# Attention scores in one run per kind: four heads' exponentials first, four heads' maxima second

## The chip, the cores and the metric

The kernel runs on one core of one Trainium2 chip. The metric is the time of one execution in microseconds of the device, the median of several runs. Engines are named as in the profile: PE is the matrix engine, PEld its weight loads, DVE the vector engine, ACT the scalar engine, POOL the general-purpose engine, SP the queue that issues most DMAs.

## The reference

A transformer layer on `x` of shape (2, 1024, 512) in float32. First attention with 32 heads of 16 channels, then a feed-forward part with quantised weights (512 to 1376 to 512).

```python
x = x + attn(layernorm(x))      # q, k, v projections; per head:
                                #   scores = q @ k.T / 4        (1024 x 1024)
                                #   softmax(scores) @ v
                                # then the output projection w_o
x = x + ffn(layernorm(x))       # int4 input, ternary weights, relu(gate)^2 * up,
                                # int8 middle, down projection
```

Attention dominates: 2 x 32 matrices of 1024 x 1024 scores, each reduced to a softmax and multiplied with `v`.

## The kernel before

**Steps and slots.** One *step* is four heads of one batch entry and 512 queries; there are 32 steps. The four heads of a step stand in the four groups of 32 partitions (r = 0 to 3), so one head's score product has a contraction of 32 rows and uses a quarter of PE's rows. Products of different r can stand in the array at the same time. A step has eight *slots* (`NT = 8`), and the loop at L1400 goes through all slots of all steps, one slot T after the other.

**The scores are computed twice.** Once with queries on the partitions, so that DVE can take the maximum over keys ("maxima", `max_mm` L590, tile `psm`, reduced by DVE at L600 into `pm`); ten slots later (`LE = NT + 2`) with keys on the partitions, so that ACT can take the exponential ("exponentials", `exp_mm` L630, tile `pse`, ACT at L634 into `e`). The score product of the exponentials has three passes per head: two with the query's high and low part, and one that adds the row of maxima (`mrow`, out of `onesr`). The maxima have two passes per head. A slot does one tile of each for each of the four heads. A PSUM tile `pse` or `psm` holds two heads (128 x 1024 float32): j = 0 holds r = 0 and 1, j = 1 holds r = 2 and 3.

**The order of PE's work in a slot** is the order in which the program is written (manual schedule; each engine runs its instructions in order):

1. `scores(...)`, the *first run*,
2. `weigh_values` (L660): the exponentials of the slot before times `v`, eight matmuls,
3. `fill.run(100.0, short=True)`: light steps of other work, hardly ever a matmul,
4. `scores(...)`, the *second run*,
5. in the second slot of a step `max_rows` (L613, tile `psn`): the step's maxima turned into a row,
6. `fill.run(...)`: the *filler*, matmuls of the projections, the output projection and the feed-forward part, by a budget that is fixed when the program is built.

`scores` allocates its tiles and mixes the passes of both kinds:

```python
es = [(*x, scores_psum(f"pse_{x[0]}_{x[1]}_{x[2]}")) for x in exps]
ms = [(*x, max_tile(*x)) for x in maxs]
for l in range(3):
    for x in es:
        exp_mm(*x, l)
    if l or not es:
        for x in ms:
            max_mm(*x, l - bool(es)) if l - bool(es) < 2 else None
for x in es:
    exponentials(*x)      # ACT, L634
for x in ms:
    max_reduce(*x)        # DVE, L600
```

**Before the change**, a slot with both kinds ("mixed") makes its first run of the exponentials with j = 0 and the maxima with j = 1, and its second run of the exponentials with j = 1 and the maxima with j = 0. Each run has one tile for ACT and one for DVE. The slots T = 0 to 9 have maxima alone and the last ten have exponentials alone; those make one run of four heads.

**PSUM.** `scores_psum` takes from a pool of three tiles of two banks each (`ps_s`, `bufs=3`), in turn: each tile takes the place of the one three allocations earlier, and its first matmul waits until that one has been read. `psn` takes from the same pool. The filler has one bank of its own (`ps_o`), the accumulator of `weigh_values` another (`ps_a`).

**Other DVE and ACT work** stands in the same in-order queues, behind the filler matmuls that feed it: normalisation, quantisation of weights and activations, products of the feed-forward part. In the first slot of a step DVE also does `max_parts` (L605 to L608).

Of the kernel before, what the change touches and what calls it, by code (L numbers as in the profile page):

```python
# [233 lines left out]
def kernel(  # L234
# [101 lines left out]
    def scores_psum(name):  # L336
        return ps_s.tile([P, 2, QB], F32, tag="s", name=name)
# [224 lines left out]
    def places(n):  # L562
        kst[n] = sb.tile([P, S], F32R, tag="kst", name=f"kst_{n}", bufs=3)
        qst[n] = [sb.tile([P, QB], F32R, tag="qst", name=f"qst_{n}_{l}", bufs=6) for l in range(2)]

    def load_k(n, first=0):
        nc.sync.dma_start(kst[n][:, first:].bitcast(F32), step_k(n)[:, :, first:])

    def load_q(n):
        b, h, g, s = steps[n]  # L570
        for l, q in enumerate(qst[n]):
            rows = qD[b, g, h][l].rearrange("(r s e) q -> s r e q", r=4, s=2)[s]
            nc.sync.dma_start(q.bitcast(F32), rows)

    def load_v(n):
        b, h, g, s = steps[n]
        vt[n] = sb.tile([P, NT, 4, 32], F32, tag="v", name=f"v_{n}", bufs=2)
        nc.sync.dma_start(vt[n].rearrange("p t r e -> p (t r e)"), vD[b, g, s].rearrange("p t e -> p (t e)"))

    def max_tile(n, i, j):  # L580

        if i == 0 and n not in pm:
            pm[n] = sp.tile([P, TQ, 2, 4], F32, tag="pm", name=f"pm_{n}")
        return scores_psum(f"psm_{n}_{i}_{j}")

    def max_mm(n, i, j, ps, l):
        kh, t = divmod(i, TQ)
        for r in (2 * j, 2 * j + 1):
            rows = slice(32 * r, 32 * r + 32)
            nc.tensor.matmul(  # L590
                ps[:, r % 2, :],
                qst[n][l][rows, t * P : (t + 1) * P],
                kst[n][rows, kh * QB : (kh + 1) * QB],
                start=(l == 0),
                stop=(l == 1),
            )

    def max_reduce(n, i, j, ps):
        kh, t = divmod(i, TQ)
        nc.vector.tensor_reduce(pm[n][:, t, kh, 2 * j : 2 * j + 2], ps, AX.X, ALU.max, negate=True)  # L600

    def max_parts(n):
        m = sp.tile([P, TQ, 4], F32, tag="m", name=f"m_{n}")
        p = pm.pop(n)
        nc.vector.tensor_tensor(m, p[:, :, 0, :], p[:, :, 1, :], ALU.min)  # L605
        cols = mcols[n % 2].rearrange("p t (r c) -> p t r c", r=4)
        nc.vector.tensor_copy(cols[:, :, :, 0], m)
        nc.vector.tensor_tensor(cols[:, :, :, 1], m, cols[:, :, :, 0].bitcast(F32), ALU.subtract)  # L608
# [12 lines left out]
    def exp_mm(n, i, j, ps, l):  # L621
        for r in (2 * j, 2 * j + 1):
            rows = slice(32 * r, 32 * r + 32)
            if l < 2:
                left, right = kst[n][rows, i * P : (i + 1) * P], qst[n][l][rows, :]
            else:

                rows = slice(32 * r, 32 * r + 2)
                left, right = onesr[rows, :], mrow[n][rows, :]
            nc.tensor.matmul(ps[:, r % 2, :], left, right, start=(l == 0), stop=(l == 2))  # L630

    def exponentials(n, i, j, ps):
        e = sb.tile([P, 2, QB], F32, tag="e", name=f"e_{n}_{i}_{j}", bufs=4)
        nc.scalar.activation(e, ps, AF.Exp, scale=SCALE)  # L634
        probs.setdefault((n, i), {})[j] = e

    def scores(exps, maxs):
# [11 lines that stand above are left out]
            exponentials(*x)  # L649
        for x in ms:  # L650
            max_reduce(*x)
# [3 lines left out]
    def weigh_values(n, i):  # L655
        if i == 0:
            acc[n] = ps_a.tile([P, QB], F32, tag="a", name=f"pso_{n}")
        e = probs.pop((n, i))
        for r in range(4):
            nc.tensor.matmul(  # L660
                acc[n][32 * r : 32 * r + 32, :],
                vt[n][:, i, r, :],
                e[r // 2][:, r % 2, :],
                start=(i == 0),
                stop=(i == NT - 1),
            )
        if i == NT - 1:
            po[n] = sb.tile([P, QB], F32, tag="po", name=f"po_{n}", bufs=3)
            nc.scalar.copy(po[n], acc[n])

    def normalise(n):


        b, h, g, _ = steps[n]
        p0, p1 = po.pop(n - 1), po.pop(n)
        dD = dram.tile([4, 2, QB], F32, name=f"dD_{n}")
        rD = dram.tile([4, 2, QB], F32, name=f"rD_{n}")
        yield ("gap", 3)
        for s, p in enumerate((p0, p1)):
            nc.sync.dma_start(dD[:, s, :], p[16 * (1 - s) :: 32, :])  # L680
        yield ("gap", 4)
        k = 8 * QB // P
        den = sp.tile([P, k], F32, tag="den", name=f"den_{n}", bufs=2)
        nc.sync.dma_start(den, bass.AP(dD.tensor, dD.offset, [[k, P], [1, k]]))
        yield ("gap", 6)
        for c in (slice(0, QB // 2), slice(QB // 2, QB)):
            nc.vector.copy_predicated(p0[:, c], second.to_broadcast([P, QB // 2]), p1[:, c])
            yield ("gap", 1)
        nc.vector.reciprocal(den, den)
        yield ("gap", 2)  # L690
        nc.sync.dma_start(bass.AP(rD.tensor, rD.offset, [[k, P], [1, k]]), den)
        yield ("gap", 3)
        rden = sb.tile([P, QB], F32, tag="rden", name=f"rden_{n}", bufs=1)
        nc.sync.dma_start(
            rden, bass.AP(rD.tensor, rD.offset, [[QB, 8], [0, 16], [1, QB]])
        )
        yield ("gap", 4)
        OT[b, h, g] = sb.tile([P, QB], F32, tag="OT", name=f"OT_{b}_{h}_{g}", bufs=5)
        nc.gpsimd.tensor_tensor(OT[b, h, g], p0, rden, ALU.mult)  # L699
# [617 lines left out]
    def load_slot(n):  # L1317

        return NT * n - (4 if n == 2 else 5)
# [5 lines left out]
    def due_v(n):  # L1325
        return NT * n + (8 if n < 8 else 5)
# [64 lines left out]
    def feed():  # L1391

        while ffns and set(ffns[0][2]) <= fill.done | {ffns[0][2][0]}:
            name, gen, after, due, cost, by = ffns.popleft()
            fill.add(name, gen, after, "ffn", due, cost, by)
# [4 lines left out]
    for T in range(LE + NT * NSTEP + 1):  # L1400
        fill.slot = T
        ne, ie = divmod(T - LE, NT)
        nm, im = divmod(T, NT)
        nw, iw = divmod(T - LE - 1, NT)

        fill.scores = int(T < LE - 1 or T >= NT * NSTEP)

        n = T // NT + 1
        if 1 < n < NSTEP and T == load_slot(n):
            b, h, g, s = steps[n]  # L1410
            fill.ensure(f"k_{b}_{g}_0", f"k_{b}_{g}_1", f"q_{b}_{g}_{h}")
            places(n)
            load_k(n)
            load_q(n)
        n = (T - 5) // NT
        if 0 <= n < NSTEP and T == due_v(n):
            b, h, g, s = steps[n]
            fill.ensure(f"v_{b}_{g}_0", f"v_{b}_{g}_1")
            load_v(n)
        if im == 0 and 0 < nm <= NSTEP:  # L1420
            max_parts(nm - 1)
        exps = [(ne, ie, j) for j in range(2)] if 0 <= ne < NSTEP else []
        maxs = [(nm, im, j) for j in (1, 0)] if nm < NSTEP else []
        mixed = bool(exps and maxs)
        if mixed:
            scores(exps[:1], maxs[:1])
        elif exps:
            scores(exps, [])
        if 0 <= nw < NSTEP:
            weigh_values(nw, iw)  # L1430
            if iw == NT - 1 and nw % 2 and nw < NSTEP - 1:
                b, h, g, _ = steps[nw]
                fill.add(f"norm_{b}_{h}_{g}", normalise(nw), (), "back")
            if iw == NT - 1 and nw == NSTEP - 2:
                fill.add("tokens", first_tokens(nw), (), "ffn", 0)
        feed()
        fill.run(100.0, short=True)
        if mixed:
            scores(exps[1:], maxs[1:])
        elif maxs:  # L1440
            scores([], maxs)
        if im == 1 and 0 < nm <= NSTEP:
            max_rows(nm - 1)
        share = min(max(fill.pace([w[4:] for w in ffns]), SHARE), MORE)
        left = fill.run(share + min(left, SHARE))
# [52 lines left out]
```

## Time and profile before

| | |
|---|---|
| time, three runs | 1177.97, 1178.94, 1180.83 us; median 1178.94 |
| profiled execution | span 1179.7 us from first to last instruction; the page gives no other time of it |
| PE busy | 1154.8 us, 98% of the span |
| DVE busy | 868.8 us, 74% |
| ACT busy | 686.8 us, 58% |
| POOL busy | 264.1 us, 22% |
| granted PE clock | 0.999 (mean) |

In the timeline a line gives start, length, engine, line of the kernel, instruction, tile written <- tiles read, shapes and number of instructions merged; the bracket is the idle time of the engine before it and what ended it. A matmul's length contains the time in which the next ones already run, so intervals are read from start to start.

### The profile page before, as it was taken

What the parts mean: (1) busy time and instruction counts of PE and PEld (TensorE: products, weight loads), DVE (VectorE), ACT (ScalarE), POOL (GpSimd) and SP (SyncE); (2) the same over time, 40 slices, a digit from 0 to 9 for tenths busy, and PEclk for the clock granted to TensorE, in tenths of its full rate; (3) what the DMA queues carried; (4) which work ended last, traced back from release to release, by engine and by line L of the source; (5) the groups of instructions that cost most, each with busy time, mean ns of one, the idle gap of its engine ahead of it and who ended that gap; (6) DMA issues with size and microseconds to landing.
All of it is one profiled execution on the core that took longest, in us unless ns stands there. A gap on an engine that the chain in (4) does not pass through costs nothing.

```text
span 1179.7 us, 21990 instructions
## 1 busy us (share of the span) xinstructions
PE 1154.8 (98%) x8922; PEld 522.5 (44%) x8922; DVE 868.8 (74%) x1261; ACT 686.8 (58%) x878; POOL 264.1 (22%) x319
## 2 busy tenths in 40 slices
PE   8899999999999999999999999999999999999998
PEld 5454444544444444544444445444444433444344
DVE  6765577898876677788866665786988788888467
ACT  2058765556565556566665555465666555665746
POOL 3224336465501101221011011022110001220111
PEclk9999999999999999999999999999999999999999
DMA  5666765556623323443633324244442516362300
GB/s 157 174 183 194 249 197 176 172 190 197 194 93 96 103 55 110 113 95 77 94 86 121 124 59 147 84 130 138 84 97 60 89 53 83 58 81 55 79 9 37
DMA packets 97099, 135.35 MB, mean 115 GB/s; under 512 B 34829, under 2 KB 54285, under 8 KB 96997
## 3 DMA queue, kind: packets, MB, share of 16 engines
q1 hardware_dynamic: 87204, 105.75, 34.6%
q0 software_dynamic: 9792, 28.19, 7.7%
q8 instruction: 70, 1.15, 0.4%
q14 instruction: 33, 0.26, 0.1%
HBM read 89.25 MB, written 37.19 MB: 107 GB/s over the span
## 4 chain that ended last, share of the span: by engine, by line
PE 81%; DVE 5%; DMA 5%; issue 2%; POOL 2%; SPq 2%; ACT 2%; POOLq 0%; DVEq 0%; ACTq 0%
PE pse L630 25%; PE pso L660 18%; PE psm L590 9%; PE psv L533 4%; PE psk L476 4%; PE psy L847 4%; PE psq L476 4%; PE pu L937 2%; PE py L1006 2%; DVE pm L600 2%; PE pg L937 2%; DMA rden<-rD 1%; PE psn L613 1%; SPq L505 1%; PE end L1161 1%
## 5 line engine op out<-in xcount | busy, mean ns | idle before, releaser
L600 DVE TENSOR_REDUCE pm<-psm 128x2 f32<-128x1024 f32 x512 | 623.8, 1222 | 242.9 <-PE pse L630 146.0
L634 ACT ACTIVATE e<-pse 128x1024 f32<-128x1024 f32 x512 | 522.7, 1023 | 408.2 <-PE pse L630 307.3
L590 PE MATMUL psm<-kst,qst 32*128 32x512 f32 x2048 | 369.5, 444 | 7.3 <-DMA kst<-kD 3.8
L630 PE MATMUL pse<-qst,kst 32*128 32x512 f32 x2048 | 367.6, 442 | 3.9 <-DVE pm L600 3.1
L630 PEld LDWEIGHTS pse<-qst,kst 32*128 32x128 f32 x2048 | 149.2, 183 | 332.8 <-issue 199.7
L660 PE MATMUL pso<-e,v 128*32 128x512 f32 x2048 | 272.9, 605 | 0.0
L630 PE MATMUL pse<-mrow,onesr 2*128 2x512 f32 x1024 | 203.9, 396 | 0.0
L590 PEld LDWEIGHTS psm<-kst,qst 32*128 32x128 f32 x2048 | 151.3, 183 | 25.5 <-ACT e L634 10.8
L630 PEld LDWEIGHTS pse<-mrow,onesr 2*128 2x128 f32 x1024 | 94.5, 183 | 3.3
L951 POOL TENSOR_TENSOR g<-g 128x460 f32<-128x460 f32 (+1 forms) x36 | 34.7, 964 | 244.7 <-ACT g L947 237.4
L660 PEld LDWEIGHTS pso<-e,v 128*32 128x32 f32 x2048 | 40.4, 108 | 94.4 <-issue 93.7
L807 POOL TENSOR_SCALAR low<-raws,whalf 128x512 bf16<-128x512 f32 (+2 forms) x35 | 52.0, 1488 | 30.5 <-DMA raws<-in_wuT 8.1
L476 PE MATMUL psq<-xnT,wq 128*128 128x512 f32 x112 | 57.8, 626 | 0.0
L533 PE MATMUL psv<-wv,xnT 128*128 128x128 f32 x384 | 53.2, 285 | 0.0
L533 PEld LDWEIGHTS psv<-wv,xnT 128*128 128x128 f32 x384 | 45.9, 191 | 12.5 <-issue 11.7
L847 PE MATMUL psy<-wo,OT 128*128 128x512 f32 x96 | 49.6, 625 | 0.0
L476 PE MATMUL psk<-xnT,wk 128*128 128x512 f32 x96 | 49.5, 624 | 0.0
L699 POOL TENSOR_TENSOR OT<-po,rden 128x512 f32<-128x512 f32 x15 | 19.2, 1278 | 99.5 <-PE pse L630 52.8
L547 POOL DMA_DIRECT2D vD<-vst x30 | 16.7, 559 | 110.5 <-ACT vst L545 107.8
L909 POOL TENSOR_SCALAR xn<-x,mv,a 128x512 f32<-128x512 f32 x12 | 25.1, 2089 | 71.5 <-DVE a L885 71.5
L937 PEld LDWEIGHTS <-xqT 128*128 128x128 bf16 x288 | 22.4, 98 | 37.8 <-issue 23.8
L937 PE MATMUL pg<-wg,xqT 128*128 128x460 fp8e4 (+1 forms) x144 | 34.2, 360 | 0.0
(227 smaller groups left out, 945.1 us busy)
## 6 DMA issues: line engine op xcount, KB each, us to landing
v<-vD SPq DMA_DIRECT2D x32, 512.0 KB
kst<-kD SPq DMA_DIRECT2D x31, 512.0 KB
qst<-qD SPq DMA_DIRECT2D x60, 256.0 KB
vD<-vst POOLq DMA_DIRECT2D x30, 256.0 KB, 5.7
qD<-hi_q SPq DMA_DIRECT2D x28, 256.0 KB
qD<-lo_q SPq DMA_DIRECT2D x28, 256.0 KB
x<-in_x SPq DMA_DIRECT2D x20, 256.0 KB
rden<-rD SPq DMA_DIRECT2D x15, 256.0 KB
```

The source lines that it names most:

```text
L476: nc.tensor.matmul(ps, w[:, c, :], xnT[b, h][:, c, :], start=(c == 0), stop=(c == KC - 1))
L533: nc.tensor.matmul(ps[:, i * P : (i + 1) * P], xnT[b, half][:, c, i * P : (i + 1) * P], w[:, c, :], start=(c == 0), stop=(c == KC - 1),)
L590: nc.tensor.matmul(ps[:, r % 2, :], qst[n][l][rows, t * P : (t + 1) * P], kst[n][rows, kh * QB : (kh + 1) * QB], start=(l == 0), stop=(l = ...
L600: nc.vector.tensor_reduce(pm[n][:, t, kh, 2 * j : 2 * j + 2], ps, AX.X, ALU.max, negate=True)
L630: nc.tensor.matmul(ps[:, r % 2, :], left, right, start=(l == 0), stop=(l == 2))
L634: nc.scalar.activation(e, ps, AF.Exp, scale=SCALE)
L660: nc.tensor.matmul(acc[n][32 * r : 32 * r + 32, :], vt[n][:, i, r, :], e[r // 2][:, r % 2, :], start=(i == 0), stop=(i == NT - 1),)
L807: nc.gpsimd.tensor_scalar(low, w, h[:rows, m, 1:2], None, ALU.is_lt)
L847: nc.tensor.matmul(ps, OT[b, h, g][:, i * P : (i + 1) * P], wo[g], start=(g == 0), stop=(g == NG - 1),)
L909: nc.gpsimd.tensor_scalar(xn, xt, mean, a, ALU.subtract, ALU.mult)
L937: nc.tensor.matmul(ps, xT[:, c, :], w[:, c, n : n + size], start=(c == 0), stop=(c == KC - 1))
L951: nc.gpsimd.tensor_tensor(g2[j], g2[j], g2[j], ALU.mult)
```

## The change

A mixed slot no longer mixes. Its first run is all exponentials of the slot (j = 0 and 1, four heads, three passes: twelve matmuls), its second run all maxima (j = 1 and 0, four heads, two passes: eight matmuls). The instructions are the same and as many; their order in PE's, ACT's and DVE's queues and the turn of the PSUM tiles change. Slots with one kind alone are as before.

```diff
         exps = [(ne, ie, j) for j in range(2)] if 0 <= ne < NSTEP else []
         maxs = [(nm, im, j) for j in (1, 0)] if nm < NSTEP else []
-        mixed = bool(exps and maxs)
-        if mixed:
-            scores(exps[:1], maxs[:1])
-        elif exps:
+        if exps:
             scores(exps, [])
         if 0 <= nw < NSTEP:
             weigh_values(nw, iw)
...
         feed()
         fill.run(100.0, short=True)
-        if mixed:
-            scores(exps[1:], maxs[1:])
-        elif maxs:
+        if maxs:
             scores([], maxs)
         if im == 1 and 0 < nm <= NSTEP:
             max_rows(nm - 1)
```

## The prediction

> **What bounds the kernel now.** I read the page first (busy times, chain, groups), then the timeline of an ordinary mixed slot, then the two ends of the loop, where runs of one kind already stand.
>
> ```profile
> PE 1154.8 (98%) x8922; PEld 522.5 (44%) x8922; DVE 868.8 (74%) x1261; ACT 686.8 (58%) x878; POOL 264.1 (22%) x319
> ...
> L600 DVE TENSOR_REDUCE pm<-psm 128x2 f32<-128x1024 f32 x512 | 623.8, 1222 | 242.9 <-PE pse L630 146.0
> L634 ACT ACTIVATE e<-pse 128x1024 f32<-128x1024 f32 x512 | 522.7, 1023 | 408.2 <-PE pse L630 307.3
> ```
>
> PE is the bound: it hardly pauses and holds 81% of the chain of waits, while DVE and ACT sit idle 243 and 408 us before their score work, mostly for PE (the last two columns). The timeline of one slot, PE's lines alone (start, length), shows what a run costs:
>
> ```profile
> 504.84 0.50 PE L630 MATMUL pse<-qst,kst 32*128 32x512 f32 x2
> 504.97 0.50 PE L590 MATMUL psm<-kst,qst 32*128 32x512 f32 x2
> 505.18 0.40 PE L630 MATMUL pse<-qst,kst 32*128 32x512 f32 x2
> 505.31 0.40 PE L590 MATMUL psm<-kst,qst 32*128 32x512 f32 x2
> 505.41 0.40 PE L630 MATMUL pse<-mrow,onesr 2*128 2x512 f32 x2
> 505.74 0.95 PE L937 MATMUL pg<-wg,xqT 128*128 128x460 fp8e4 x4
> 506.62 0.74 PE L630 MATMUL pse<-qst,kst 32*128 32x512 f32 x4
> ...
> 507.64 1.07 PE L660 MATMUL pso<-e,v 128*32 128x512 f32 x8
> 508.63 0.50 PE L630 MATMUL pse<-qst,kst 32*128 32x512 f32 x2
> ```
>
> Start to start: run 0.90, filler 0.88, run 1.02 (some 0.1 of it a maximum that waits for its tile, which ACT had read at 506.93), values 1.00: 3.80 us. In a run the exponentials' three passes set the length (0.34, 0.23 and 0.34 to the next work); the maxima of the other two heads lie beside two of them. Each run leaves two quarters of the array unused in one pass. Runs of one kind, at the start of the loop:
>
> ```profile
> 43.27 0.74 PE L590 MATMUL psm<-kst,qst 32*128 32x512 f32 x8
> ...
> 43.94 1.98 PE L476 MATMUL psk<-xnT,wk_first 128*128 128x512 f32 x4
> 44.04 2.36 DVE L600 TENSOR_REDUCE pm<-psm 128x2 f32<-128x1024 f32 x2 [0.41 <-PE psm L590]
> ```
>
> and, at the end:
>
> ```profile
> 1095.03 0.74 PE L630 MATMUL pse<-qst,kst 32*128 32x512 f32 x8
> ...
> 1095.60 0.41 PE L630 MATMUL pse<-mrow,onesr 2*128 2x512 f32 x4
> ...
> 1095.94 1.06 PE L660 MATMUL pso<-e,v 128*32 128x512 f32 x8
> ...
> 1096.10 1.94 ACT L634 ACTIVATE e<-pse 128x1024 f32<-128x1024 f32 x2 [0.30 <-PE pse L630]
> ```
>
> All maxima take PE 0.67, all exponentials 0.91: four heads' passes run as fast as two heads'. But the two reductions then follow each other on DVE (2.36), the two exponentials on ACT (1.94).
>
> **What PE saves.** The median runs are 0.905 and 0.908 (242 clean ones of each, start to start). 0.91 + 0.67 = 1.58 instead of 1.81, -0.23 a slot; against the mean of both with their waits (1.91 in short slots, 1.84 in long) -0.33 and -0.26. The Trainium skill, "TensorEngine Tiling (Array Packing)", section "Theoretical Speedup", counts a contraction of 32 as fourfold: five passes instead of six would make 1.51 of 1.81, an estimate. Its section "PSUM Bottleneck" speaks against the change: after such a gain the emptying of PSUM may bind, and both ScalarE and VectorE should share it; now each run has one emptying engine. Taken at its hardest (the two engines never overlapping) that would make 2.36 + 1.94 = 4.30 a slot, an estimate, and +70 over 160 short slots; no run here shows it yet.
>
> **The wait that it adds.** With four tiles a slot and three places the turn is E0(k) after E1(k-1), E1(k) after M1(k-1), M1(k) after M0(k-1), M0(k) after E0(k) (E: exponentials, M: maxima, digit: j, k: slot; the pool of three is taken in turn). So E1 waits until DVE has reduced the M1 of the run just before, and M0 until ACT has read the E0 of the run just before. PE is in order: behind E1's first pass stand both tiles' later passes and the values; behind M0's, the filler. From the start of the second run, called 0 here:
> - run start to first reduction 0.77 (43.27 to 44.04), reduction 1.22, release 0.05 (a DVE end at 47.27, its PE waiter at 47.32): E1 starts at 2.04.
> - E1's first pass to the last pass of E0 0.34, to ACT 0.50 (1095.60 to 1096.10), exponential 1.02, release 0.05: M0 at 3.95.
> - On PE: passes 0.34 + 0.23 + 0.34, values 1.00, from 2.04: the next second run at 3.95.
>
> Both ways close at 3.95, whatever the filler, if it is done by 2.04. PE's own work is 2.58 plus the filler. Fillers under 1.37 therefore no longer set the slot; longer ones still do. DVE's second reduction is done at 0.77 + 2.36 = 3.13 and its next is due at 3.95 + 0.77 = 4.72, so 1.59 of other DVE work fits between.
>
> In the slot with psn that tile takes a place and the turn shifts by one: the next E0 waits for M1 and E1 for M0, the later reduction. 0.77 + 2.36 + 0.05 + 0.91 + 1.00 = 5.09. The trace of before has no slot in which E1 waits so; below, its bounds are these 5.09 and PE's own 2.58 + 0.50 (psn) + 0.89 (filler) = 3.97, and I take the upper one, since both reductions stand in a row at 44.04.
>
> **The sum.** The 244 mixed slots of the timeline, from one first L660 to the next:
> - 160 with a filler under 1.2 (mean 0.95), mean 3.86: to 3.95, +14.4.
> - 54 longer (two of 1.4, 36 of 1.9, 16 of 2.8), mean run time 1.84: to 1.58, -14.0. After a long filler E0 starts together with E1 and M0 is late: 0.34 + 0.23 + 0.50 + 1.02 + 0.05 = 2.14 against 0.91 + 1.00 on PE, 0.23; the next short slot absorbs it, since it counts from M1. A second long slot would not; I add nothing and put 3 into the upper end.
> - 26 with psn and a short filler, mean 4.33: to 5.09, +19.8.
> - 4 with psn and a long filler (5.2 to 6.1): -1.
> - DVE's other work: between the second reductions of neighbouring slots it sums to 0.84 in the mean; 48 slots have more than 1.59, by 26.2 in all. Where a long filler or psn widens the slot part of it fits; 19.5 in 32 slots is left. The excess delays M1's reduction and so everything. Durations of neighbours overlap by 0.04 to 0.08, so I take +16; ends 0 and 26.
>
> +35 on the span of 1179.7: 1215. The median of the runs is 0.8 under that span, so about 1214.
>
> ACT has 2.0 us between a slot's second exponential and the next first one for 0.57 of other work (mean); its copies and relus are hidden there, and 2 to 3 us would come of the first 20 slots, where it has 1.5 to 2.7. No DMA is moved past another. The first ten slots and the last ten keep their order: nothing. The filler's bank is emptied later where DVE empties it (behind both reductions, at about 3.8), but the next filler starts at 4.6: nothing; without that cover it would be up to 0.7 in some 70 slots.
>
> The clock: the trace's only mid-kernel half clock follows a PE wait of 3.80 us for a DMA (at 55.69; mean granted clock 0.60 from 56.4 to 60.6). The new waits are 0.4 to 1.2 us; the nearest rows as short (0.73 at 47.32) kept 1.00. So I price it at nothing. The Trainium skill, "TensorE: Matmul & The Clock Gate", Part 1, puts the half clock behind an idle window of some 3.4 us; by it too the term is nothing.
>
> **Rivals.**
> - *Faster: the tiles come free in time.* Every slot then keeps PE's gain: 186 short and psn slots by 0.33, 58 by 0.26: -76, about 1103. It needs M1 reduced by 1.55, when a filler of 0.88 ends, instead of 2.04. For it: 98% PE. Against it: 0.77 + 1.22 stand in the trace, and with three places there is none to wait in. Each 0.1 us of the loop is worth 18.6 us over 186 slots; the loop would have to be 3.76 with my DVE term, 3.85 without, for no change. Chance 0.10 for anything faster by over 0.3%.
> - *No change*, a loop of 3.85 with the DVE excess hidden: 1179. 0.04.
> - *Much slower: DVE's queue.* If its other work waits for filler results that come late and so stands in front of M1's reduction in more than the 32 slots: half of its 0.84 in 244 slots is 102, about 1300; a quarter about 1250. For it: slices in which DVE is at 8 tenths. Against it: most of it is ready while PE waits. 0.08 beyond 1243.
> - *The change doesn't do what it says*: four heads don't run side by side. Both ends of the loop show that they do; under 0.02, in the above.
>
> **How the numbers follow.** The forecast's own bounds: below, a loop 0.05 shorter (-9) and no DVE excess (-16), 1189; above, a loop 0.05 longer (+9), the full excess (+10), long slots in a row (+3) and ACT's term (+3), 1239. If psn slots came halfway between their bounds it were 15 less than 1214, inside. I open the range a little on both sides, 1186 to 1243, with 0.76 in it. Outside: 0.08 above (the queue), 0.02 from 1182.5 to 1186, 0.04 within 0.3% of 1178.9, 0.10 below that. 0.3%, 3.5 us, is about what a measurement of this kernel tells from no change. So faster 0.10, same 0.04, slower 0.86.
>
> **What would show it.** Right: slots with short fillers at 3.95 and alike; PE idle before L630 put down to DVE pm L600, some 0.4 in each (70 us in all, against 30 now), before L590 to ACT e L634; psn slots at 5.1; PE's busy share down to some 92%; pure runs of 0.91 and 0.67. Wrong: slots of 3.5 with short fillers (the tiles were free), or E1 released later than 2.04 after the second run's start with DVE busy on other lines (the queue).

## The result and the profile after

The changed kernel took 1195.45 us (median of four runs, 1193.72 to 1200.71). The kernel before took 1178.83 us beside it, so the ratio is 1.0141 (95% interval 1.0115 to 1.0167). The change makes the kernel 16.6 us slower. The forecast was 1214 in a range of 1186 to 1243: the direction and the range held, but the loss is just under half of the +35 that the sum gave. The profiled execution had a span of 1198.9 us, 19.2 more than the one of before. The sum was made for that span. But the profiled execution is the slowest of the four (1200.71 us, mean granted clock 0.994); the other three took 1193.72 to 1197.12 at 0.999 to 1.000.

The page of the changed kernel (busy times, then the two groups of instructions that empty the score tiles):

```profile
PE 1167.7 (97%) x8922; PEld 508.4 (42%) x8922; DVE 855.3 (71%) x1261; ACT 668.7 (56%) x878; POOL 270.3 (23%) x319
...
L600 DVE TENSOR_REDUCE pm<-psm 128x2 f32<-128x1024 f32 x512 | 602.8, 1219 | 285.0 <-PE psm L590 284.7
L634 ACT ACTIVATE e<-pse 128x1024 f32<-128x1024 f32 x512 | 496.5, 1022 | 376.3 <-PE pse L630 376.2
```

One reduction (1219 ns) and one exponential (1022 ns) cost what they did. PE still counts as 97% busy, because a matmul's length runs on while the next ones start; a wait inside a run hides in those lengths. So the loop can't be read from busy shares. It is read from the timeline of an ordinary slot of the changed kernel (start, length; the bracket is the idle time before and what ended it):

```profile
512.78 0.76 PE L590 MATMUL psm<-kst,qst 32*128 32x512 f32 x8
...
513.48 0.95 PE L937 MATMUL pg<-wg,xqT 128*128 128x460 fp8e4 x4
513.56 2.36 DVE L600 TENSOR_REDUCE pm<-psm 128x2 f32<-128x1024 f32 x2 [1.59 <-PE psm L590]
...
514.36 1.21 PE L630 MATMUL pse<-qst,kst 32*128 32x512 f32 x8
...
514.84 0.29 PEld L630 LDWEIGHTS pse<-qst,kst 32*128 32x128 f32 x6 [0.29 <-DVE pm L600]
...
515.18 0.62 PE L630 MATMUL pse<-mrow,onesr 2*128 2x512 f32 x4
515.69 1.94 ACT L634 ACTIVATE e<-pse 128x1024 f32<-128x1024 f32 x2 [0.67 <-PE pse L630]
515.73 1.06 PE L660 MATMUL pso<-e,v 128*32 128x512 f32 x8
516.73 0.77 PE L590 MATMUL psm<-kst,qst 32*128 32x512 f32 x8
```

From 512.78 to 516.73 is 3.95, the forecast loop. The run of maxima gives way to the filler after 0.70, and the filler is done at 514.36, and then E1 waits for DVE, and behind E1's first pass everything but the first two of the exponentials' eight score products (the x6 in the row of weight loads): the first reduction ends at 513.56 + 1.22 = 514.78, and the weights of E1 load at 514.84. The run is done at 515.73 instead of 514.36 + 0.91 = 515.27. This wait of 0.46 is more than the 0.23 that PE saves. The bracket on DVE, 1.59, is the free time that the prediction worked out.

All 244 mixed slots, the same slot by its number against before, by the prediction's classes (us, measured in two profiled executions of the changed kernel):

| class | predicted | first profile | second profile |
|---|---|---|---|
| 160 short | +14.4 | +19.2 | +20.2 |
| DVE's other work | +16 | in the rows above | in the rows above |
| 54 long | -14.0 | -1.6 | -5.8 |
| 26 psn, short | +19.8 | +3.2 | +2.4 |
| 4 psn, long | -1 | +0.4 | +0.4 |
| ahead of the first slot | 0 | -2.0 | +2.0 |
| sum (spans) | +35 | +19.2 | +19.1 |

The short slots went to a median of 3.95 (mean 3.98) and the long ones from a median of 4.72 to 4.63. The psn slots went to a mean of 4.46, not 5.09.

### The profile page after: what moved, and what is told of

Same layout as the page of the kernel before. It is cut to its first block, busy times and chain, and to the rows that moved or that the text cites. A ratio compares the mean times of both kernels' runs of the same rounds, so it can differ in the third digit from the quotient of the medians.

```text
span 1198.9 us, 22022 instructions
## 1 busy us (share of the span) xinstructions
PE 1167.7 (97%) x8922; PEld 508.4 (42%) x8922; DVE 855.3 (71%) x1261; ACT 668.7 (56%) x878; POOL 270.3 (23%) x319
## 4 chain that ended last, share of the span: by engine, by line
PE 71%; DVE 8%; issue 7%; POOL 4%; DMA 4%; ACT 3%; SPq 1%; POOLq 0%; ACTq 0%; DVEq 0%
PE pse L630 18%; PE pso L660 15%; PE psm L590 12%; DVE pm L600 4%; PE psv L533 4%; PE psy L847 4%; PE psk L476 4%; PE psq L476 3%; PE py L1006 2%; ACT e L634 2%; PE pu L937 2%; PE pg L937 2%; POOL low L807 1%; PE psn L613 1%; DMA rden<-rD 1%
## 5 line engine op out<-in xcount | busy, mean ns | idle before, releaser
L600 DVE TENSOR_REDUCE pm<-psm 128x2 f32<-128x1024 f32 x512 | 602.8, 1219 | 285.0 <-PE psm L590 284.7
L634 ACT ACTIVATE e<-pse 128x1024 f32<-128x1024 f32 x512 | 496.5, 1022 | 376.3 <-PE pse L630 376.2
L660 PE MATMUL pso<-e,v 128*32 128x512 f32 x2048 | 273.3, 606 | 0.0
L630 PE MATMUL pse<-qst,kst 32*128 32x512 f32 x2048 | 241.2, 452 | 8.0 <-DVE pm L600 6.8
L590 PE MATMUL psm<-kst,qst 32*128 32x512 f32 x2048 | 221.4, 447 | 6.5 <-ACT e L634 3.3
L590 PEld LDWEIGHTS psm<-kst,qst 32*128 32x128 f32 x2048 | 103.1, 184 | 224.1 <-DVE pm L600 52.7
L630 PEld LDWEIGHTS pse<-qst,kst 32*128 32x128 f32 x2048 | 104.6, 183 | 157.2 <-issue 87.5
L630 PE MATMUL pse<-mrow,onesr 2*128 2x512 f32 x1024 | 135.8, 393 | 0.0
L660 PEld LDWEIGHTS pso<-e,v 128*32 128x32 f32 x2048 | 40.4, 108 | 95.5 <-issue 91.4
L630 PEld LDWEIGHTS pse<-mrow,onesr 2*128 2x128 f32 x1024 | 77.2, 184 | 7.3
L937 PE MATMUL pu<-wu,xqT 128*128 128x460 fp8e4 (+1 forms) x144 | 34.1, 360 | 0.0
## 6 DMA issues: line engine op xcount, KB each, us to landing
qst<-qD SPq DMA_DIRECT2D x60, 256.0 KB
vD<-vst POOLq DMA_DIRECT2D x30, 256.0 KB, 6.2
qD<-hi_q SPq DMA_DIRECT2D x28, 256.0 KB
qD<-lo_q SPq DMA_DIRECT2D x28, 256.0 KB
x<-in_x SPq DMA_DIRECT2D x20, 256.0 KB
rden<-rD SPq DMA_DIRECT2D x15, 256.0 KB
```

Of the source, the lines that this page charges most:

```text
L590: nc.tensor.matmul(ps[:, r % 2, :], qst[n][l][rows, t * P : (t + 1) * P], kst[n][rows, kh * QB : (kh + 1) * QB], start=(l == 0), stop=(l = ...
L660: nc.tensor.matmul(acc[n][32 * r : 32 * r + 32, :], vt[n][:, i, r, :], e[r // 2][:, r % 2, :], start=(i == 0), stop=(i == NT - 1),)
L937: nc.tensor.matmul(ps, xT[:, c, :], w[:, c, n : n + size], start=(c == 0), stop=(c == KC - 1))
```

## The experiments

E, M and the digits are those of the prediction. F is a slot's filler. A slot is counted from one first L660 to the next. "Changed" is the changed kernel, "before" the one before.

### 1. The changed kernel again

No edit; the question was whether one slot of 10.05 us in the first profile (below) explains the short slots.

> The changed kernel once more, unaltered, for an undisturbed profile. The profile of the first run holds one slot of 10.05 us (at 133.8), in which ACT waits for a weight tile's DMA with two exponentials queued behind, PE idles 2.2 us and the granted clock drops. Theory (the loop through three PSUM places sets 3.95 in slots with short fillers): 1192 to 1196, median slot with a short filler again 3.95, psn slots 4.4. Rival (the loss is such disturbances, clock and DMA): without the slot of 10.05 the slots with short fillers would come near the 3.86 of before and the time near 1180.

Measured: 1200.44 (1198.69 to 1203.56) beside 1180.39 for before on this chip, ratio 1.0172 (1.0136 to 1.0209), which overlaps the first interval. The slot of 10.05 was 6.41 here, and the short slots still had their median at 3.95 and took 20.2 more in all. So the loop, not a disturbance, carries the loss. The time missed its expectation by 4 to 8 us, 1.6 of that from this chip's before; the ratio is what compares.

### 2. The places strictly in turn

The prediction took the three places in turn. Here the program is made to do so:

```diff
-    ps_s = ctx.enter_context(tc.tile_pool(name="ps_s", bufs=3, space=PSUM))
+    ps_s = ctx.enter_context(tc.tile_pool(name="ps_s", bufs=1, space=PSUM))
...
+    def turned(name, shape, dtype=F32):
+        turn[0] += 1
+        return ps_s.tile(shape, dtype, tag=f"s{turn[0] % 3}", name=name)
```

> The three PSUM places of the scores are taken strictly in turn (three tags with one buffer each) instead of by the pool's choice. In the slot with psn E1 then waits for the later reduction M0, as the prediction assumed. Theory (the prediction's psn term failed because the pool gives E1 the place that psn leaves, not M0's): the 26 psn slots with short fillers go from 4.46 to 5.09, all others stay, so 16 us more than e1: about 1210. Rival (the psn slots were mis-sized for another reason: DVE's second reduction is out of the way in time, or E1 never waits for M0): within 3 us of e1.

Measured: 1216.28 (1214.72 to 1223.45), ratio 1.0315 (1.0274 to 1.0356): 15.8 more than the changed kernel on the same chip, where 16 were expected. The short slots stayed at a median of 3.95. The psn slots took a median of 5.10, mean 5.21 (4.43 in experiment 1). The same psn slot in both timelines, the changed kernel first:

```profile
505.04 2.36 DVE L600 TENSOR_REDUCE pm<-psm 128x2 f32<-128x1024 f32 x2 [1.50 <-PE psm L590]
...
505.40 0.66 PE L613 MATMUL psn<-identr,mcols 128*128 128x128 f32 x4 [0.18 <-ACT e L634]
...
506.10 0.58 ACT L617 CAST mrow<-psn 128x512 fp32r<-128x512 f32 x1 [0.75 <-PE psn L613]
...
506.91 0.74 PE L630 MATMUL pse<-qst,kst 32*128 32x512 f32 x8
```

and strictly in turn (its lines are numbered six higher):

```profile
507.26 2.36 DVE L606 TENSOR_REDUCE pm<-psm 128x2 f32<-128x1024 f32 x2 [1.49 <-PE psm L596]
...
509.13 1.27 PE L636 MATMUL pse<-qst,kst 32*128 32x512 f32 x8
...
509.67 0.30 PEld L636 LDWEIGHTS pse<-qst,kst 32*128 32x128 f32 x6 [0.36 <-DVE pm L606]
```

Strictly in turn, E1 starts at 509.67, after the second reduction (507.26 + 2.36 = 509.62). In the changed kernel the eight score products run from 506.91 without a wait (0.74), while the second reduction runs until 507.40: E1 does not use M0's place. It has the one that psn leaves when ACT's copy ends at 506.68. Here the pool handed out the place that came free earlier. So the "in turn" that the kernel's description gives, and the prediction built on, does not hold where psn comes in.

### 3 and 4. Half the reduction

DVE's maxima go over half of the keys only, so one reduction is shorter and the rest is unchanged; once in the changed kernel and once in before, as control:

```diff
-        nc.vector.tensor_reduce(pm[n][:, t, kh, 2 * j : 2 * j + 2], ps, AX.X, ALU.max, negate=True)
+        nc.vector.tensor_reduce(
+            pm[n][:, t, kh, 2 * j : 2 * j + 2], ps[:, :, : QB // 2], AX.X, ALU.max, negate=True
+        )
```

> The changed kernel with each maximum taken over half of its keys (DVE reads 256 of every 512 columns). The softmax is the same for any such row constant. A reduction should take some 0.65 instead of 1.22. Theory (E1 waits for M1's reduction): E1 is released at 1.47 after the second run instead of 2.04, before a filler of 0.95 ends; what then holds is M0's wait for ACT, slot = filler + 2.81 = 3.76 in the 160 short slots, -35 us, and about 1156 in all; L630's waits for DVE pm vanish. Rival (PE's own runs, the clock or ACT alone set the time): within 5 us of e1.

> The kernel before with the same halved maxima, as the control for e3. Theory: there the reductions lie beside the exponentials on ACT and PE hardly waits for DVE (some 30 us of waits in all are put down to pm), so 1168 to 1179, at most 10 us less than before. Rival (DVE's load as such costs time in both orders): the same gain as e3, 35 us or more.

Measured: changed 1173.16 (1168.05 to 1176.02), ratio 0.993 (0.9905 to 0.9955), 27 less than with the full reduction; before 1176.31 (1174.77 to 1182.01), ratio 0.9972 (0.9953 to 0.999), 4 less. The group of the changed kernel with half the reduction, and its PE timeline over one slot:

```profile
L600 DVE TENSOR_REDUCE pm<-psm 128x2 f32<-128x512 f32 x512 | 329.8, 686 | 507.8 <-PE psm L590 507.7
```

```profile
505.28 0.97 PE L590 MATMUL psm<-kst,qst 32*128 32x512 f32 x8
506.19 0.95 PE L939 MATMUL pg<-wg,xqT 128*128 128x460 fp8e4 x4
507.06 0.74 PE L632 MATMUL pse<-qst,kst 32*128 32x512 f32 x8
...
507.98 1.07 PE L662 MATMUL pso<-e,v 128*32 128x512 f32 x8
508.97 0.97 PE L590 MATMUL psm<-kst,qst 32*128 32x512 f32 x8
```

The reduction takes 686 ns, and the wait of E1 is gone: the eight score products run from 507.06 without one, and the exponentials' run takes 0.92. DVE's link is thus what held the slot at 3.95. But the slot is 3.69 and not 2.58 + 0.88 = 3.46: the run of maxima takes 0.91 to the filler (505.28 to 506.19) instead of 0.67. M0 waits in it for ACT, which reads E0 0.23 too late. As the slots stand now, each one is its filler plus 2.81 (3.69 with 0.88, 3.87 with 1.06). The short slots came out at 3.78 in the mean where 3.76 was expected. The total is 17 above its expectation. Some 9 of that is that the expectation went by about 1191 for the changed kernel (1156 + 35), which took 1200.4 on this chip; most of the rest is in the long slots, which rose from a mean of 4.88 in experiment 1 to 4.97, one of them 8.00. The psn slots took 4.47, no less than with the full reduction. With half the reduction the changed order is 0.7% faster than the kernel before, and before's own order 0.3%.

### 5, 6 and 7. Half the exponentials, and half of both

ACT makes the exponentials of half of the queries, and the values read that half twice; in 6 the reduction is halved as well, and 7 is before with both halves.

```diff
+        half = slice(0, QB // 2)
-        nc.scalar.activation(e, ps, AF.Exp, scale=SCALE)
+        nc.scalar.activation(e[:, :, half], ps[:, :, half], AF.Exp, scale=SCALE)
...
-                e[r // 2][:, r % 2, :],
+                e[r // 2][:, r % 2 : r % 2 + 1, : QB // 2].to_broadcast([P, 2, QB // 2]),
```

> The changed kernel with each exponential over half of its columns (256 of every 512); the values then read that half twice, so PE's work is the same and the output is not the layer's. An exponential should take some 0.6 instead of 1.02. Theory (two links, of which the one over DVE alone holds the short slots): M0 comes free before PE gets to it, but E1 still waits for M1's reduction, so slots with short fillers stay at 3.95; long ones lose their wait for M0 (4.88 to filler + 2.58 = 4.73, -8 us) and psn slots theirs (4.43 to about 4.1, -9): 17 us less than the changed kernel. Rival (it is ACT, which now has its two exponentials in a row, that holds the short slots): 3.8 or less there, 30 us less or more.

> The changed kernel with halved maxima and halved exponentials (the output is not the layer's). Theory: with both links short PE's own work is left, 2.58 + filler: 3.53 in slots with short fillers, 4.73 in long ones, about 4.0 with psn; -73 - 8 - 11: some 92 us less than the changed kernel, about 1105. Rival (runs of one kind cost PE more than the pure runs at the loop's ends showed, or PE's clock falls): short slots no shorter than the 3.69 to 3.87 of the halved maxima alone, 1160 or more.

> The kernel before with the same two halvings, as the control for e6 (the output is not the layer's). Theory: mixed runs cost PE 1.81 a slot whatever the emptying; without waits 2.81 + filler: 3.76, 4.96 and 4.20 instead of 3.86, 4.99 and 4.33, some 21 us less than before: about 1158, and so 50 us slower than e6: the change is then what it says. Rival (the gain of e6 is the lighter emptying and not PE's passes): within 15 us of e6.

Measured: half the exponentials 1181.27 (1178.82 to 1187.56), ratio 1.0012 (0.9996 to 1.0029), by the ratios 19 less than experiment 1 where 17 were expected; half of both 1114.04 (1112.12 to 1116.94), ratio 0.9447 (0.9424 to 0.947), 9 above its expectation; before with half of both 1157.33 (1155.63 to 1157.76), ratio 0.9809 (0.9792 to 0.9827), as expected.

With ACT's link cut alone, the timeline of the changed kernel shows that E1 still waits for DVE:

```profile
505.88 1.06 PE L661 MATMUL pso<-e,v 128*32 128x512 f32 x8
...
506.88 0.74 PE L590 MATMUL psm<-kst,qst 32*128 32x512 f32 x8
...
507.66 2.36 DVE L600 TENSOR_REDUCE pm<-psm 128x2 f32<-128x1024 f32 x2 [1.59 <-PE psm L590]
...
508.94 0.29 PEld L630 LDWEIGHTS pse<-qst,kst 32*128 32x128 f32 x6 [0.32 <-DVE pm L600]
...
509.83 1.06 PE L661 MATMUL pso<-e,v 128*32 128x512 f32 x8
```

The slot is 3.95 again (505.88 to 509.83), and E1's weights load 0.06 after the first reduction's end (507.66 + 1.22). The short slots kept their median of 3.95. So of the two ways round the loop that the prediction closed at 3.95, the one through DVE and PE holds it alone, with ACT's cut. What did fall is the long slots, to F + 2.57, and the psn slots, to F + 3.07 (mean 4.07): these are PE's own 2.58, and the prediction's lower bound for psn, 2.58 + 0.50 + F. Their surplus in the changed kernel was waits for ACT.

With both cut, PE's saving is there at last. The groups and the timeline of half of both:

```profile
L600 DVE TENSOR_REDUCE pm<-psm 128x2 f32<-128x512 f32 x512 | 329.9, 686 | 447.2 <-PE psm L590 447.0
L637 ACT ACTIVATE e<-pse 128x512 f32<-128x512 f32 x512 | 277.8, 594 | 444.4 <-PE pse L632 444.2
```

```profile
504.19 0.74 PE L590 MATMUL psm<-kst,qst 32*128 32x512 f32 x8
504.86 0.95 PE L940 MATMUL pu<-wu,xqT 128*128 128x460 fp8e4 x4
505.74 0.74 PE L632 MATMUL pse<-qst,kst 32*128 32x512 f32 x8
...
506.64 1.06 PE L663 MATMUL pso<-e,v 128*32 128x512 f32 x8
507.64 0.74 PE L590 MATMUL psm<-kst,qst 32*128 32x512 f32 x8
```

The maxima take 0.67, the exponentials 0.90 and the values 1.00, together 2.57, and the slot 3.45. Before with both halves stands at F + 2.80 (3.68), so the change gains 0.23 in an ordinary slot, 43 us in all (1157.33 to 1114.04). The gain that the prediction counted on PE is real, but with whole tiles to empty the loops take it all.

### 8. Another order

The filler comes between the exponentials and the maxima, and the values behind the maxima:

```diff
             scores(exps, [])
+        share = min(max(fill.pace([w[4:] for w in ffns]), SHARE), MORE)
+        left = fill.run(share + min(left, SHARE))
+        if maxs:
+            scores([], maxs)
+        if im == 1 and 0 < nm <= NSTEP:
+            max_rows(nm - 1)
         if 0 <= nw < NSTEP:
             weigh_values(nw, iw)
...
         fill.run(100.0, short=True)
-        if maxs:
-            scores([], maxs)
-        if im == 1 and 0 < nm <= NSTEP:
-            max_rows(nm - 1)
-        share = min(max(fill.pace([w[4:] for w in ffns]), SHARE), MORE)
-        left = fill.run(share + min(left, SHARE))
```

> The changed kernel with the filler moved between the two runs and the values behind the maxima: exponentials, filler, maxima, values. Each link then spans another piece of PE's work: M0's wait spans the filler, E1's the values. Theory: E1 to the next E1 is 0.91 + filler + 2.04, so a slot is filler + 2.95: 3.83 with a feed-forward filler of 0.88, 4.00 with a projection of 1.05 (3.95 both in the changed kernel), 5.10 instead of 4.88 in long ones, about 4.3 with psn; -13 + 12 - 3: within 8 us of the changed kernel, but with slots of these lengths. Rival (a slot has a floor of 3.95 that the order of PE's work doesn't move, such as ACT's and DVE's work for it): 3.95 or more everywhere.

Measured: 1225.24 (1216.95 to 1226.16), ratio 1.0367 (1.0324 to 1.041), 25 more than experiment 1 by the medians. The expectation missed. PE's timeline:

```profile
502.47 1.11 PE L630 MATMUL pse<-qst,kst 32*128 32x512 f32 x8
...
503.75 1.16 PE L533 MATMUL psv<-wv,xnT 128*128 128x128 f32 x8
504.84 0.74 PE L590 MATMUL psm<-kst,qst 32*128 32x512 f32 x8
505.51 1.06 PE L660 MATMUL pso<-e,v 128*32 128x512 f32 x8
506.50 1.13 PE L630 MATMUL pse<-qst,kst 32*128 32x512 f32 x8
```

Here M0 no longer waits (0.67), but only the values (1.00) lie between the maxima and E1, 1.67 against the 2.04 that DVE needs. So the exponentials' run takes 1.28, and every slot is F + 2.95: 3.83 with a filler of 0.88, 4.01 with 1.06, a median of 4.87 for the long ones. The loop behaved as worked out, while the rest did not. Against experiment 1, by class and in the mean: 23 psn slots with a short filler took 4.91 instead of 4.43 (+11; an estimate of 4.3 stood behind the expectation), 7 with a long one, among them one of 9.16 us, 6.04 instead of 5.37 (+5), the long slots F + 2.86 instead of F + 2.71 (+7), the few with hardly any filler +2, the start +3; the 60 slots with 0.88 win back only 0.07 each (-4). That is 24 of the 24.8 by which the two profiles' spans differ. Part of it is the clock and not the order. Four slots lie at a granted clock of 0.50 for most of their length: the one of 9.16, whose filler took 4.67 where six such matmuls take 2.77 elsewhere, and from 1037.6 three of 5.35, 5.84 and 5.13 where some 3.9 is usual; 7 to 8 us in all, an estimate from these. Three of the four runs had a mean granted clock of 0.987 or 0.988; the fourth, at 0.995, took 1216.95. So about 16 of the 25 are the order's own, still outside the 8 that were expected.

### 9 and 10. A longer filler

Two more matmuls of 0.19 in each of 72 products of the feed-forward part, results overwritten, in changed and in before:

```diff
+            for _ in range(2):
+                nc.tensor.matmul(ps, xT[:, 0, :], w[:, 0, n : n + size], start=True, stop=True)
             for c in range(KC):
```

> The changed kernel with two matmuls more (0.19 each, the first matmul of the group done beforehand, then overwritten) in each of the 72 gate and up fillers of the loop: 0.39 us of PE work more in 72 slots, 59 of them without psn and with nothing else. Theory (short slots are held by the loop over DVE and ACT, PE idles in them): 2.57 + 1.27 = 3.84 is still under 3.95, so those 59 slots stay at 3.95; psn slots and the rest pay 13 x 0.39: 5 us more than the changed kernel. Rival (PE at 97% busy is still the bound): 28 us more.

> The kernel before with the same matmuls added, as the control for e9. Theory (PE is the bound there; a slot is 2.81 + filler, plus 0.11 of waiting for ACT where the filler is 0.88): the 59 slots go from 3.80 to 4.08, the others pay 0.39: 59 x 0.28 + 13 x 0.39, 22 us more than before, about 1201, level with e9. Rival (PE has the same slack there): within 8 us of before.

Measured: changed 1212.68 (1211.5 to 1213.79), ratio 1.0272 (1.0254 to 1.029); before 1198.69 (1196.36 to 1198.91), ratio 1.0147 (1.0125 to 1.0169). For before that is 18 more where 22 were expected: its 59 ordinary slots of this kind went from 3.80 to 4.08, all of it. For changed it is 12 more by the ratios of this experiment and of experiment 1 (1.0272 against 1.0172), where +5 was expected by the theory and +28 by the rival that PE is the bound: neither is right. By the medians the 59 slots went from 3.95 to 4.08 (59 x 0.13 = 7.7), 8 psn slots with this filler from 4.26 to 4.82 (4.5). Changed with the longer filler, PE's timeline:

```profile
521.12 0.96 PE L590 MATMUL psm<-kst,qst 32*128 32x512 f32 x8
522.02 0.56 PE L937 MATMUL pg<-wg,xqT 128*128 128x456 fp8e4 x2
522.41 0.93 PE L939 MATMUL pg<-wg,xqT 128*128 128x456 fp8e4 x4
523.28 0.74 PE L630 MATMUL pse<-qst,kst 32*128 32x512 f32 x8
...
525.17 0.97 PE L590 MATMUL psm<-kst,qst 32*128 32x512 f32 x8
```

The filler is 1.27 (522.02 to 523.28) and E1 doesn't wait. In exchange E0 starts with E1, and then M0 waits for ACT: the maxima take 0.90 (521.12 to 522.02) in slot after slot, and the slot is 1.27 + 2.81 = 4.08 (4.05 in the one shown). The expectation had left this second wait out. So the loop gives way at a filler of 3.95 - 2.81 = 1.14, not at 1.37.

## Why the prediction came out as it did

The mechanism of the short slots held. Three terms of the sum did not: psn, DVE's other work and the long slots.

**Right: the bound moves, and the loop of 3.95.** The 160 short slots have it as their median, both of its ways can be followed in the timeline, and halving the reduction, which was the theory's link, frees it. The rule of "PSUM Bottleneck" in the Trainium skill's "TensorEngine Tiling (Array Packing)" was the right warning: this case's runs agree in kind (half the reduction -27 us, half of both -86 us). At its hardest, 4.30 a slot, it was too harsh, since both engines overlap within a slot: 3.95 was measured.

**Failed: the psn term, +19.8 predicted, +3.2 and +2.4 measured.** The step "that tile takes a place and the turn shifts by one: the next E0 waits for M1 and E1 for M0" took the pool to go strictly in turn, and its upper bound followed. The price was right for that case: strictly in turn gave a median of 5.10 for 5.09 and +15.8 us. But the changed kernel gives E1 the place that psn leaves. Its 4.43 lies 0.46 above the lower bound of 3.97; 0.36 of that is waits for ACT, since half the exponentials bring it to 4.07.

**Failed: the term for DVE's other work, +16 predicted, about 5 measured.** What the short slots have over 3.95 is 19.2 - 14.4 = 4.8 in the first profile and 5.8 in the second. Of the 160, 147 stand within 0.05 of 3.95; 13 others, up to 0.58 over it, carry the excess. The step that failed is "the excess delays M1's reduction and so everything". Looked up slot by slot in the profile of before, only 11 of the prediction's 32 stretches, with 6.4 of its 19.5 us, delay the E1 of a short slot. The other 21 come ahead of a long or a psn slot, where PE has other work while the reduction is late; one of these, at 252.7 in the first profile, took 1.6 more, and most of the others show nothing of it. Operations that overlap are not the error: counted once, the stretches come to the 16 that the prediction took, and those ahead of short slots to 5.4, close to what was measured.

**Failed the other way: the long slots, -14.0 predicted, -1.6 and -5.8 measured.** 46 of the 54 follow a short slot, and their median went from F + 2.80 to F + 2.61: -0.19 each, not -0.26. The 0.26 had come from the runs' mean with their waits. Of the eight that follow a psn or a long slot five gained nothing (F + 2.80 to F + 2.83), because M0's wait of 0.23 was not absorbed. The prediction had named this for a second long slot and put it at nothing in the sum. The 0.23 are absorbed only where the E1 of the run ahead has waited, which brings E0 ahead of it: with half the reduction (experiment 3), where E1 no longer waits, the long slots have their median at F + 2.81. More than half of what is missing lies in single slots: in the first profile the one of 10.05 us (+4.5), the one at 252.7 (+1.6, the DVE stretch above) and one at half clock (+1.3), which are 7.5 of the 12.4.

**Errors that offset each other.** In the first profile the psn term was 16.6 too large and the one for DVE's other work 11 too large, while the gain of the long slots was 12 too large; these leave 15 of the 16 between +35 and +19.2. So the range held in part by luck: some 28 us of loss that did not come were in part made up for by a gain that did not come either, and some of that was single waits and the clock.

**Signs that were wrong.** PE idle before L630 for DVE pm L600 was to be some 70 us:

```profile
PEld pse L630 <- DVE pm L600: 41.3, 97, 2.0
...
PE pse L630 <- DVE pm L600: 6.8, 17, 1.6
```

In the view of waits of the changed kernel it is 48 (31 in before), and PE's busy share is 97%, not 92%. M0's waits for ACT hardly appear in that view at all; where M0 does wait, it is seen in the length of the maxima's run, 0.90 instead of 0.67.

**The formula that the runs leave.** A changed slot takes 3.95 or F + 2.81, whichever is longer, and a long slot behind a waiting short one F + 2.61. A slot of before takes F + 2.81 too, up to 0.11 more with a filler of 0.88. So the 0.23 that PE saves come back as M0's wait even where E1's isn't met, and short fillers pay the floor of 3.95 on top.

**The clock** was priced at nothing. For the loop that is right: the ordinary slot above stands at 3.95 with a granted clock of 1.00. For the total it is not. In one slot of the first profile ACT's queue held a step of weight preparation (L768) that waited 2.02 for its data, the slot's exponentials stood behind it, and PE stood still behind those. In PE's timeline, then in the windows (length; busy us of PE, PEld, DVE, ACT and POOL; granted clock, DMA share, GB/s):

```profile
134.77 0.49 PE L590 MATMUL psm<-kst,qst 32*128 32x512 f32 x2
137.42 1.22 PE L590 MATMUL psm<-kst,qst 32*128 32x512 f32 x6 [2.16 <-ACT e L634]
138.57 3.78 PE L533 MATMUL psv<-wv,xnT 128*128 128x128 f32 x16
```

```profile
134.00:138.00 4.00, 1.84 (x14) 0.69 (x8) 0.00 (x0) 2.26 (x4) 1.08 (x2) 0.86 0.74 242
138.00:142.00 4.00, 4.00 (x22) 3.43 (x16) 2.36 (x2) 0.89 (x3) 0.54 (x1) 0.50 0.66 196
```

The slot took 10.05 us instead of 5.54; 4.5 us in all. In the second profile the wait was shorter there, and the clock stayed at 1.00. The clock was also at 0.50 for 3.4 us from 1010.7 in the first profile (a slot of 6.61, 5.08 in the second) and from 259.3 in the second (6.13, 4.51 in the first), about 1.5 us each time. The loop of before had no such place in its profile. In the three other runs of the result, at a clock of 0.999 to 1.000, the change cost 15 to 18 us, so most of the loss is not the clock.

## What to carry to other kernels

Before work is regrouped so that a unit is packed better, write down the loop of each buffer (who fills it, who empties it, whose place the next tile takes) and add it up beside the unit's own work: here PE's 2.58 plus the filler could not be reached, because the loop over one reduction (0.77 + 1.22 + 0.05) and PE's passes behind it (1.91) needed 3.95. Here two engines that empty tiles side by side (3.80 a slot) beat each having its own turn (3.95), although PE then packs worse. More places or smaller tiles were not tried. And find out which place a pool really hands out before pricing a wait on it: strictly in turn or not was 16 us here.

## What was unexpected in the hardware

The granted clock fell to 0.50 far more easily than the prediction had it, and no length of pause divides the cases. In the loops of these profiles it stayed there for about 3.4 us or a multiple of it, up to 13.7.

| | PE pause before (us) | where |
|---|---|---|
| half clock within 4 us of the pause's start | 2.16; 2.23; 1.52; 1.39; 1.42; 1.42 and 1.07 | changed; experiments 9; 4; 3; 1; 5 |
| no half clock | 1.64; 1.36; 1.41; 1.42 | changed at 256.0; experiments 1 at 138.6; 2 at 255.1; 9 at 256.5 |
| half clock, no pause over 0.64 in the 8 us before | - | changed at 1010.7; experiments 2 at 996.0 and 1033.5; 8 at 164.3 and 1038.1; 9 at 1018.2 |

The Trainium skill, "TensorE: Matmul & The Clock Gate", Part 1, puts the drop behind an idle window of about 3.4 us; all these pauses were shorter, so here the measurement decides. In experiment 8 the DMA engines moved 393 to 420 GB/s as the clock fell at 164.3, but at 1010.7 of the changed kernel they moved nothing, so DMA traffic is not what the falls have in common. What sets them off stays open.
